# When the zeros of a score table start, and what the first gather of each beat waits for

## The chip, the cores and the metric

The kernel runs on one core of a Trainium2 chip. The metric is the device time of one execution in microseconds (us). The kernel before takes 2227.58 us, the median of three runs (2226.61 to 2228.72). Of one further execution there is a hardware profile: that execution took 2228.76 us, and 2227.0 us lie between its first and its last instruction (the span). Times within the profile count from the start of the span.

The engines are called by their short names: PE multiplies matrices (TensorE), DVE is the vector engine, ACT the scalar engine, POOL is GpSimd, and SP only starts transfers. DMAs are started from the queues of SP, ACT and POOL.

## The reference

Two layers over a graph of 625 nodes, 10000 directed edges and 1024 features. Layer 0 adds to `x` a graph attention, a linear attention and a quantised feed-forward block; layer 1 is a two-step graph aggregation, another linear attention, a softmax attention and a mixture of eight experts. The change touches only the graph attention of layer 0:

```python
loop = jnp.arange(n, dtype=edge_index.dtype)
src = jnp.concatenate([edge_index[0], loop])
dst = jnp.concatenate([edge_index[1], loop])
xl = (x @ Wl).reshape(n, H, D)          # H = 4 heads of D = 64
xr = (x @ Wr).reshape(n, H, D)
msg = xl[src] + xr[dst]
act = jnp.where(msg > 0, msg, NEG_SLOPE * msg)
e = jnp.einsum('ehd,hd->eh', act, att)
m = jax.ops.segment_max(e, dst, num_segments=n)
p = jnp.exp(e - m[dst])
denom = jax.ops.segment_sum(p, dst, num_segments=n)
alpha = p / (denom[dst] + 1e-16)
out = jax.ops.segment_sum(alpha[..., None] * xl[src], dst, num_segments=n)
out = out.reshape(n, HID)
return out @ W_up
```

Each edge needs a row of `xl` and a row of `xr` (256 numbers each), chosen by its two node numbers, and gives four scores.

## The kernel before

**The score table.** A tensor `table` in DRAM has a row of four scores for every pair of nodes. It is first filled with zeros by one DMA of 6160 KB on SP's queue (L404), out of a tile `none` that POOL has set. Each edge's four exponentiated scores are later scattered to its pair's row, and the 625 diagonal rows are written for the self loops (`self_loops`, L647, ten small DMAs on ACT's queue). When all that is done, `load_table` (L827) reads the table back in five blocks `tb`, DVE multiplies them by the edge counts `CT` (`weigh`, L841), and PE multiplies the result by the rows `xl1` (`sums`, tile `pg`).

**The projections.** For each of five blocks of 125 nodes, `left_right` (L540) multiplies the node features by `Wl` and `Wr`. ACT copies the result to `xlr` and stores its left half to `xl_d` from its own queue and its right half to `xr_d` from POOL's queue. `rows_dma` (L171) makes two DMAs of each store, for 112 and for 13 rows.

**The beats.** The edges lie in 79 columns of up to 128. Two columns make a group, so there are 40 groups, numbered 0 to 39 (the last is one column of 16 edges). `one_beat` (L684) writes out the work of one beat g:

- up to four gathers on POOL for group g: for each column j one of `xl_d` into `ga` and one of `xr_d` into `gb` (`gather`, L605). Both tiles have five buffers, so group g needs the buffers of group g-5;
- on DVE the scores of group g-4 (`score_group`, four instructions: add, L591, L592 and L594), and on ACT the exponential of group g-5;
- on POOL two scatters for group g-6 (`scatter`, L626), which stand between the gathers.

At the end, `lags[:] = 1, 1, 2` (L807) shortens these distances: from beat 36 on there are four scatters in a beat, and DVE scores up to group g-1. The scatters that are left after beat 39 follow on their own. A scatter also waits until the scatter before it has landed, since both write the table.

**The order.** PE, DVE, ACT, POOL and SP each run their instructions in the order in which the program writes them out. `work(us)` (L702) counts estimated PE time and writes out a beat whenever enough has gone by (8.6 us for a beat from beat 7 on). In between stand the two linear projections `pk`, `pv`, the count matmuls `pct`, the queries `pq` and, last, the output products `px` (`mixed`). Before the last beats DVE sums weights for the quantiser (`weight_sums`, L767), and among them it rounds the weights (`ternary`, L782 to L785).

**The pace.** `group` and the other matmul helpers note their newest matmul in `latest["pe"]` (L131). `behind` (L135) adds a semaphore wait by hand. The first gather of each beat waits with it for that matmul:

```python
                    if j == 0 and side == 0 and "pe" in latest:
                        behind(got, latest["pe"])
```

**SP's queue.** SP starts the loads of `x`, the weights `wd` and `wlr`, the biases, the two halves of `Wk`, then the zeros (L404) and the two halves of `Wv` (L121). The next transfer behind these is a bias of the second half (L237), which waits for DVE until 158 us.

Of the kernel before, what the change touches and what calls it, by code (L numbers as in the profile page):

```python
# [20 lines left out]
NT = 5  # L21
P = 125
# [20 lines left out]
def gps_kernel(tc: tile.TileContext, w: dict, out: bass.AP):  # L43

    again = attempt(tc, w, out, False)
    with tc.If(again > 0):
        attempt(tc, w, out, True)  # L50
# [3 lines left out]
def attempt(ctx: ExitStack, tc: tile.TileContext, w: dict, out: bass.AP, shifted: bool):  # L54

    nc = tc.nc
# [6 lines left out]
    def ps1(name):  # L63
        pool, n = psums[-1]
        return pool.tile([128, 512], FP, tag="ps1", name=name, bufs=n)
# [61 lines left out]
    def group(dst, pairs):  # L127

        for i, (lhsT, rhs) in enumerate(pairs):
            made = nc.tensor.matmul(dst, lhsT=lhsT, rhs=rhs, start=(i == 0), stop=(i == len(pairs) - 1))  # L130
        latest["pe"] = made.ins.name  # L131

    latest = {}

    def behind(ins, name):  # L135

        tc.add_manual_dep(ins.ins, name, mybir.DependencyInfo(mybir.DependencyClass.Sync,
                                                              mybir.DependencyReason.DATA), reason="pace")
        return ins
# [30 lines left out]

    def rows_dma(eng, dst, src):  # L171

        eng.dma_start(out=dst[0:112], in_=src[0:112])
        eng.dma_start(out=dst[112:P], in_=src[112:P])


    graph = ctx.enter_context(ExitStack())
# [41 lines left out]
    def mid(shape, name):  # L219
        return midp.tile(shape, FP, tag="mid", name=name)  # L220
# [135 lines left out]
    with ExitStack() as st0:  # L356
# [4 lines left out]
        table = dram.tile([128 * 3080, 4], FP, name="table")  # L361
# [3 lines left out]
        with ExitStack() as edges:  # L365
# [4 lines left out]

            xin = big.tile([P, NT, D], FP, tag="big", name="xin")
            rows_dma(nc.sync, xin[:, 0, :], xrows[0])

            si = pool.tile([128, EN], I32, name="si")
            di = pool.tile([128, EN], I32, name="di")
            rw = pool.tile([128, KC], FP, name="rw")
            nc.scalar.dma_start(out=rw, in_=w["rms_w"])
            rows_dma(nc.sync, xin[:, 1, :], xrows[1])
            wd = wpool.tile([128, KC, 256], FP, tag="w", name="wd")
            nc.sync.dma_start(out=wd, in_=w["W_down"].rearrange("(k p) n -> p k n", p=128))  # L380
            for t in range(2, NT):
                rows_dma(nc.sync, xin[:, t, :], xrows[t])
# [5 lines left out]
            def load_edges():  # L388
                for dst, name in ((si, "src"), (di, "dst")):
# [8 lines left out]
            none = pool.tile([128, 440], FP, name="none")  # L398
# [2 lines left out]
                                  lambda us: work(us), nc.sync)  # L401
            lin.biases(0)
            lin.wk = Half(wpool, w["L0_Wk"], 0)
            nc.sync.dma_start(out=table.rearrange("(p a b) h -> p a (b h)", p=128, a=28),  # L404
                              in_=none.unsqueeze(1).to_broadcast([128, 28, 440]))
            lin.wv = Half(wpool, w["L0_Wv"], 0)
            sf = pool.tile([128, EN], FP, name="sf")
            df = pool.tile([128, EN], FP, name="df")
            up = pool.tile([128, EN], FP, name="up")
# [88 lines left out]
            xlr = mid([P, NT, 512], "xlr")  # L498
            xl_d = dram.tile([N, 256], FP, name="xl_d")
            xr_d = dram.tile([N, 256], FP, name="xr_d")  # L500
# [39 lines left out]
            def left_right(t):  # L540
                def pe():
                    hold["pl", t] = ps1("plr")
                    xdT = hold.pop(("xdT", t))
                    group(hold["pl", t][:P], [(xdT[:, k, :], wlr[:, k, :]) for k in range(2)])

                def after():
                    nc.scalar.activation(xlr[:, t, :], hold.pop(("pl", t))[:P], AF.Identity, scale=r0[:, t:t + 1])
                    rows_dma(nc.scalar, xl_d.rearrange("(t p) e -> t p e", p=P)[t], xlr[:, t, 0:256])
                    rows_dma(nc.gpsimd, xr_d.rearrange("(t p) e -> t p e", p=P)[t], xlr[:, t, 256:512])

                do(None, pe, after)

# [52 lines left out]
            def gather(g, j, side):  # L605
                lo, n, p = groups[g]
                if j == 0 and side == 0:
                    ab[g] = [pool.tile([128, G, 256], FP, tag=k, name=k, bufs=5) for k in ("ga", "gb")]
                if j < n:
                    src, ix = ((xl_d, si), (xr_d, di))[side]  # L610
                    got = nc.gpsimd.indirect_dma_start(  # L611
                        out=ab[g][side][0:p, j, :], out_offset=None, in_=src[:, :],
                        in_offset=bass.IndirectOffsetOnAxis(ap=ix[0:p, lo + j:lo + j + 1], axis=0))
                    if j == 0 and side == 0 and "pe" in latest:
                        behind(got, latest["pe"])

            def score_group(g):
                lo, n, p = groups[g]
# [65 lines left out]
            def one_beat():  # L684
                g = beat["g"]
                beat["g"] += 1
                if 5 <= g < NT + 5:
                    self_loops(g - 5)
                if lags[1] > lags[0]:
                    raise_all(g - lags[1])  # L690
                    scores(g - lags[0])
                else:
                    scores(g - lags[0])
                    raise_all(g - lags[1])
                for j in range(G):
                    if g < len(groups):
                        gather(g, j, 0)
                        scatter(g - lags[2] - 1)
                        gather(g, j, 1)
                    scatter(g - lags[2])  # L700
# [87 lines left out]
            for m in range(KC):  # L788
# [5 lines left out]
                if m < 3:  # L794
# [3 lines left out]
                                      in_=w[("w_gate", "w_up", "w_down")[m]].rearrange("(k p) n -> p k n", p=128))  # L798
# [418 lines left out]
    for m in range(KC):  # L1217
# [8 lines left out]
        a = m % 4  # L1226
# [48 lines left out]
    for b in range(NB_MIN, NB):  # L1275
        nc.gpsimd.dma_start(out=y_d[b * 128:(b + 1) * 128, :].rearrange("p (a n) -> p a n", a=4),
                            in_=zero.unsqueeze(1).to_broadcast([128, 4, 256]))
# [694 lines left out]
```

## Time and profile before

| what | us |
|---|---|
| median of three runs | 2227.58 |
| the profiled execution | 2228.76 |
| its span | 2227.0 |
| PE busy in the span | 2112.5 (95%) |
| DVE busy | 713.3 (32%) |
| POOL busy | 341.4 (15%) |
| ACT busy | 194.1 (9%) |
| gathers into `ga`, L611, 79 of them: busy, mean of one | 79.7, 1.009 |
| gathers into `gb`, L611, 79 of them: busy, mean of one | 81.8, 1.036 |
| scatters, L631, 79 of them: busy, mean of one | 84.2, 1.066 |
| idle time of POOL just before the `ga`, the `gb` and the scatter instructions | 74.8, 25.3, 49.4 |
| mean granted clock of PE | 0.977 |

The rows on gathers and scatters count POOL's own instruction[...]; the data land later. The usual distance between two such instructions that wait for nothing is 0.30 us, so some 24 us of each 79 are such distances and not waits. PE being busy 95% of the span says that the kernel as a whole is carried by PE. It doesn't say that PE is what ends last in every stage: what an edit in one stage is worth is read from the waits of that stage.

### The profile page before, as it was taken

How to read it: one execution, taken by the hardware profiler on the slowest of the kernel's cores; microseconds unless marked ns; L12 is line 12 of the kernel's file. 1: busy time of each engine (PE TensorE's matmuls, PEld its weight loads, DVE VectorE, ACT ScalarE, POOL GpSimd, SP SyncE). 2: the span in 40 equal slices, each digit the busy share in tenths (PEclk: the TensorE clock that was granted, in tenths of full speed). 3: DMA queues.
4: the chain of work that ended last, by engine and by line, in shares of the span. 5: the costliest groups of instructions: out<-in, count | busy, mean ns of one | idle time of the engine just before them, and what ended most of it. 6: DMA issues, size and time to landing. Idle time of an engine off the chain costs nothing. (4 is left out here: it accounts for less than half of the span.)

```text
span 2227.0 us, 17363 instructions
## 1 busy us (share of the span) xinstructions
PE 2112.5 (95%) x6934; PEld 1209.9 (54%) x6934; DVE 713.3 (32%) x1214; ACT 194.1 (9%) x354; POOL 341.4 (15%) x349
## 2 busy tenths in 40 slices
PE   8899799578899999999999999999999999999998
PEld 6466375245444777754445767557744444444443
DVE  5765467557623560000113133322011111111112
ACT  2000010001211100000000111100000000000000
POOL 1666656610000020210000000110000000000011
PEclk9999899878999999999999999999999999999999
DMA  9226252071122110231213111021099987997742
GB/s 299 77 62 209 59 182 81 25 212 33 38 85 71 52 38 1 85 142 38 76 38 104 38 38 38 20 103 61 34 347 337 331 325 282 327 331 286 275 144 92
DMA packets 145848, 301.62 MB, mean 135 GB/s; under 512 B 12370, under 2 KB 22436, under 8 KB 145754
## 3 DMA queue, kind: packets, MB, share of 16 engines
q1 hardware_dynamic: 123700, 244.23, 30.7%
q0 software_dynamic: 17376, 46.42, 7.1%
q10 hardware_dynamic: 4678, 9.72, 1.4%
q8 instruction: 58, 0.95, 0.2%
q14 instruction: 36, 0.29, 0.0%
HBM read 277.49 MB, written 22.84 MB: 135 GB/s over the span
## 5 line engine op out<-in xcount | busy, mean ns | idle before, releaser
L130 PE MATMUL pu<-w,xgT 128*128 128x512 f32 x768 | 333.9, 593 | 1.9 <-DVE xgT L1266 1.9
L130 PEld LDWEIGHTS pu<-w,xgT 128*128 128x128 f32 x768 | 144.0, 190 | 174.8 <-issue 171.7
L130 PE MATMUL pyb<-w,hb 128*128 128x512 f32 x384 | 174.3, 599 | 2.5 <-ACT yb L105 2.1
L130 PE MATMUL pq<-xnT,w 128*128 128x313 f32 x512 | 139.6, 432 | 13.8 <-DVE v L286 13.0
L130 PE MATMUL pk<-w,xnT 128*125 128x512 f32 x320 | 143.2, 599 | 3.3 <-issue 2.8
L130 PE MATMUL pv<-w,xnT 128*125 128x512 f32 x320 | 142.2, 597 | 1.5 <-issue 1.1
L130 PE MATMUL p<-tT,w 128*128 128x313 f32 x512 | 136.3, 428 | 0.4 <-DVE tT L1266 0.4
L130 PEld LDWEIGHTS pq<-xnT,w 128*128 128x128 f32 x512 | 98.2, 193 | 53.5 <-DVE v L286 13.8
L130 PEld LDWEIGHTS pyb<-w,hb 128*128 128x128 f32 x384 | 69.8, 189 | 90.9 <-issue 74.8
L1806 DVE TENSOR_TENSOR su<-pu,su 128x512 f32<-128x512 f32 x24 | 16.6, 692 | 314.6 <-ACT su L1805 314.6
L130 PEld LDWEIGHTS p<-tT,w 128*128 128x128 f32 x512 | 96.8, 190 | 37.9 <-issue 1.2
L130 PEld LDWEIGHTS pk<-w,xnT 128*125 128x125 f32 x320 | 59.8, 189 | 77.0 <-issue 76.1
L130 PEld LDWEIGHTS pv<-w,xnT 128*125 128x125 f32 x320 | 59.9, 189 | 75.4 <-issue 72.6
L1789 POOL DMA_INDIRECT xg<-rows_d,slots x12 | 11.4, 946 | 524.8 <-PE pxg L1796 449.0
L631 POOL DMA_INDIRECT table<-es,at x79 | 84.2, 1066 | 49.4 <-issue 26.2
L611 POOL DMA_INDIRECT ga<-xl_d,si x79 | 79.7, 1009 | 74.8 <-issue 33.2
L611 POOL DMA_INDIRECT gb<-xr_d,di x79 | 81.8, 1036 | 25.3 <-issue 22.8
L745 PE MATMUL px<-w,oT 128*125 128x512 f32 x160 | 69.8, 594 | 2.9 <-DVE x L909 2.0
L130 PE MATMUL px<-w,hT 128*125 128x512 f32 x160 | 70.3, 592 | 0.0
L130 PE MATMUL px<-w,oT 128*125 128x512 f32 x160 | 70.3, 592 | 0.0
L130 PE MATMUL ph<-meanT,w 128*128 128x313 f32 x256 | 70.1, 426 | 0.0
L130 PE MATMUL ph<-xnT,w 128*128 128x313 f32 x256 | 70.0, 427 | 0.0
(366 smaller groups left out, 2459.9 us busy)
## 6 DMA issues: line engine op xcount, KB each, us to landing
w<-in_eW_dram SPq DMA_DIRECT2D x144, 1024.0 KB
w<-in_L_Wk_dram SPq DMA_DIRECT2D x8, 1024.0 KB
w<-in_L_Wv_dram SPq DMA_DIRECT2D x8, 1024.0 KB
w<-in_L_Wq_dram SPq DMA_DIRECT2D x8, 1024.0 KB
w<-in_L_Wo_dram SPq DMA_DIRECT2D x8, 1024.0 KB
w<-in_W_self_dram SPq DMA_DIRECT2D x8, 1024.0 KB
w<-in_W_neigh_dram SPq DMA_DIRECT2D x8, 1024.0 KB
w<-in_sW_dram SPq DMA_DIRECT2D x8, 1024.0 KB
```

The source lines that it names most:

```text
L130: made = nc.tensor.matmul(dst, lhsT=lhsT, rhs=rhs, start=(i == 0), stop=(i == len(pairs) - 1))
L611: got = nc.gpsimd.indirect_dma_start(out=ab[g][side][0:p, j, :], out_offset=None, in_=src[:, :], in_offset=bass.IndirectOffsetOnAxis(ap=ix ...
L631: nc.gpsimd.indirect_dma_start(out=table[:, :], out_offset=bass.IndirectOffsetOnAxis(ap=at[0:p, lo + j:lo + j + 1], axis=0), in_=es[0:p, l ...
L745: made = nc.tensor.matmul(hold["px", t][:P, c, :], lhsT=oT[:, k, nodes(t)], rhs=wo[c](k), start=(k == 0), stop=(k == KC - 1 and keep is no ...
L1789: nc.gpsimd.indirect_dma_start(out=xg, out_offset=None, in_=rows_d[:, :], in_offset=bass.IndirectOffsetOnAxis(ap=slots[:, b:b + 1], axis=0))
L1806: nc.vector.tensor_tensor(su, pu[:, 0, :], su, op=ALU.mult)
```

## The change

`rows_dma` returns its two DMAs. The zeros are written out behind both halves of `Wv` on SP's queue, and they wait for the four stores of the last block of nodes (two to `xl_d`, two to `xr_d`). The first gather of a beat no longer waits for the newest matmul, but for the landing of the last gather of the beat ahead; the first gather of all waits for none.

```diff
     def rows_dma(eng, dst, src):
 
-        eng.dma_start(out=dst[0:112], in_=src[0:112])
-        eng.dma_start(out=dst[112:P], in_=src[112:P])
+        return [eng.dma_start(out=dst[lo:hi], in_=src[lo:hi]) for lo, hi in ((0, 112), (112, P))]
...
             lin.wk = Half(wpool, w["L0_Wk"], 0)
-            nc.sync.dma_start(out=table.rearrange("(p a b) h -> p a (b h)", p=128, a=28),
-                              in_=none.unsqueeze(1).to_broadcast([128, 28, 440]))
             lin.wv = Half(wpool, w["L0_Wv"], 0)
+            zeros = nc.sync.dma_start(out=table.rearrange("(p a b) h -> p a (b h)", p=128, a=28),
+                                      in_=none.unsqueeze(1).to_broadcast([128, 28, 440]))
...
                     nc.scalar.activation(xlr[:, t, :], hold.pop(("pl", t))[:P], AF.Identity, scale=r0[:, t:t + 1])
-                    rows_dma(nc.scalar, xl_d.rearrange("(t p) e -> t p e", p=P)[t], xlr[:, t, 0:256])
-                    rows_dma(nc.gpsimd, xr_d.rearrange("(t p) e -> t p e", p=P)[t], xlr[:, t, 256:512])
+                    for put in (rows_dma(nc.scalar, xl_d.rearrange("(t p) e -> t p e", p=P)[t], xlr[:, t, 0:256])
+                                + rows_dma(nc.gpsimd, xr_d.rearrange("(t p) e -> t p e", p=P)[t],
+                                           xlr[:, t, 256:512])):
+                        if t == NT - 1:
+                            behind(zeros, put.ins.name)
...
                         in_offset=bass.IndirectOffsetOnAxis(ap=ix[0:p, lo + j:lo + j + 1], axis=0))
-                    if j == 0 and side == 0 and "pe" in latest:
-                        behind(got, latest["pe"])
+                    if j == 0 and side == 0 and g:
+                        behind(got, latest["gather"])
+                    latest["gather"] = got.ins.name
```

No instruction is added or taken away on any engine; the only one that changes its place is the DMA of the zeros on SP.

## The prediction

> **What bounds the kernel now.** The page's summary puts PE at 95%, and its chain of waits names only the last matmuls, so I went to PE's timeline for holes near the edited lines, then followed the largest back over DVE and POOL.
>
> PE's timeline around 400 us:
>
> ```profile
> 394.86 27.71 PE L745 MATMUL px<-w,oT 128*125 128x512 f32 x64
> 454.23 0.68 PE L130 MATMUL pg<-xl,pT 125*125 125x65 f32 x2 [31.66 <-DVE pT L841]
> ```
>
> PE ends its projections at 422.57 and stands still for 31.66 us, until DVE has weighed the first table block. DVE's timeline:
>
> ```profile
> 388.91 0.68 DVE L621 TENSOR_TENSOR ga<-ga,gb 128x512 f32<-128x512 f32 x1
> ...
> 390.35 0.69 DVE L592 TENSOR_REDUCE es<-ga 128x8 f32<-128x512 f32 x1
> ...
> 409.76 0.69 DVE L621 TENSOR_TENSOR ga<-ga,gb 128x512 f32<-128x512 f32 x1 [7.62 <-DMA gb<-xr_d,di]
> ...
> 453.14 4.84 DVE L841 TENSOR_TENSOR pT<-tb,CT 125x500 f32<-125x500 f32 x5 [16.54 <-DMA tb<-table]
> ```
>
> DVE waits for the block's landing. POOL's timeline leads back:
>
> ```profile
> 217.02 0.97 POOL L611 DMA_INDIRECT ga<-xl_d,si  x1 [0.30 <-issue]
> ...
> 384.86 0.96 POOL L611 DMA_INDIRECT ga<-xl_d,si  x1 [8.50 <-PE px L745]
> ...
> 406.84 0.97 POOL L611 DMA_INDIRECT gb<-xr_d,di  x1 [0.30 <-issue]
> ...
> 432.64 2.31 POOL L631 DMA_INDIRECT table<-es,at  x1 [1.41 <-DMA table<-es,at]
> 436.82 0.96 POOL L631 DMA_INDIRECT table<-es,at  x1 [1.88 <-issue]
> 439.18 0.96 POOL L631 DMA_INDIRECT table<-es,at  x1 [1.39 <-DMA table<-es,at]
> 442.03 0.85 POOL L631 DMA_INDIRECT table<-es,at  x1 [1.90 <-issue]
> 444.54 0.90 POOL L173 DMA_DIRECT2D tb<-table  x1 [1.66 <-issue]
> ```
>
> So from 384.86 (the first gather of beat 36) to 444.54 POOL is the bound, and behind that hole everything follows the table: a microsecond on POOL's last scatter is one on the whole. Before 422 it is the other way round: PE has some 30 us to spare against POOL.
>
> **What the Trainium skill says.** "DMA: Bandwidth & Descriptors", section "Anatomy of one DMA", prices a DMA from POOL at about 2.0 us fixed plus its bytes, most of it the wait for the last write's receipt, and says that waits happen on the issuing sequencer. The trace agrees: the gather at 406.84 ends at 407.81, and DVE starts on it 1.95 us later. "SWDGE vs HWDGE vs iDMA" says that one DMA engine takes turns between queues, and that POOL's descriptors suffer from DVE's two-port modes; POOL's instructions of 1.5 to 2.3 us lie where DVE rounds weights (423 to 436). "TensorE: Matmul & The Clock Gate", Part 1, says that an idle PE drops to half rate; the windows show clock 0.56 at 422 to 454 and 0.50 at 454 to 470, so this rides on the hole and moves with it.
>
> **The change part by part.**
>
> *Zeros.* SP's and ACT's timelines before:
>
> ```profile
> 20.84 0.62 SPq L404 DMA_DIRECT2D table<-none  x1
> 39.30 5.45 SPq L121 DMA_DIRECT2D w<-in_L_Wv_dram  x2
> 52.19 0.31 ACTq L174 DMA_DIRECT2D xl_d<-xlr  x1
> 71.52 0.31 ACTq L173 DMA_DIRECT2D table<-own  x1
> ```
>
> The last store to `xl_d` shared a semaphore with the zeros and sat from about 46.3 until 52.19; it landed at 55.97 by the packet records, and POOL's first gather came at 57.64. Now the store takes a semaphore behind `Wv`, issues at 46.3, lands near 50, and the first gather comes at about 51.5: 6 us earlier. PE's `pv` at 55.88 waited for no load, so the earlier `Wv` gives nothing. The zeros issue near 51.5, take about 22 us (6.3 MB; 23.4 us before, from first to last packet, at 379 GB/s in all), and land at about 76. Behind them on SP stands a bias due at 158: free. ACT's diagonal store at 71.52 waits for them, some 5 us; ACT's next due work is at 81.40, so it is free, and POOL's first scatter isn't due until about 100. Bounds: nothing, up to a few us on PE if the zeros last past 81, which the later hole swallows. While they run, gathers land later: 2.7 us after POOL's end (bounds 1.5 and 4.5, what stores lagged under load), against 1.46 in quiet (packet records).
>
> *The PE wait removed.* 13 first gathers waited more than 0.34 us, summing to 45.0 us (8.50 the largest, 5.43 at 295.72); less 0.30 each, 41 us. That is what POOL gets back up to beat 36.
>
> *The landing wait added.* POOL's reaction is priced by its scatters: packets land 0.76 us after a scatter's end, the next starts 1.41 after that end when it is the only wait, and 1.88 to 1.92 when another wait is listed behind it. So POOL wakes 0.65 or 1.15 after landing. From beat 6 on, the program as built lists the landing first and DVE's buffer wait behind it: 1.46 + 1.15 = 2.61 us from the last gather's end to the next beat. A scatter stood there already: 0.30 + 0.99 + 0.30 = 1.59. Net +1.02 a beat. Unpaced beats ran 7.96 to 8.29 us (from 209.00 to 217.02: 8.02), so now 9.08.
>
> *The sum to beat 36.* Beats 0 to 2 under the zeros: four gathers, 5.0, plus 2.7 + 0.65 = 8.3 each; beats 3 to 5 about 7.1. Beat 6 starts at 51.5 + 25 + 21.5 = 98 (91.63 before). Thirty beats of 9.08 are 272. At 166 to 196, 287 to 303, near 317 and 360 weight loads fill the DMA engines (0.99 and 0.93 in the windows) and landings take 3.5 to 5 us (packet records): about four beats pay 3.3 more, 13. Beat 36 at 383, between 377 and 388, against 384.86: a gain of 2. The 41 us are nearly all given back.
>
> *The tail.* Beat 37 needs the buffers of group 32, free at 391.04, so it can't start before 391.3 (396.72 before): no gain over 5.4. From beat 36 at 383 it comes at 383 + 11.86 + 1.0 = 395.9. Beats 38 and 39 pay 1.0 each, of which the scatter chain's own 0.65 us wait behind them absorbs part: +0.8 together. The block load now lists more waits behind its scatter: +0.6 (0 to 1.2). End of table: -2 + 1 + 0.8 + 0.6 = +0.4, that is nothing. DVE scores a group four beats after its gathers, some 35 us, so it isn't held up before the tail.
>
> **The rivals.**
>
> *Unchanged (likeliest).* The PE pace goes and the landing wait takes its place at the same size: 2228.76 + 0.4, about 2229 in the profile's terms, which stands 1.2 above the median; 2227.9 beside the runs. Own range 2223 to 2232.
>
> *Faster.* POOL wakes in 0.65 rather than 1.15, or its instructions suffer less from DVE: beat 36 at about 368, and the tail stands on group 32's buffer at 391.3. Gain 5.4, less 0.2 to 1.4 for the tail; or 1.5 more, if the 1.51 us stall at 401.36 that the trace doesn't explain is gone. 2221 to 2223. For it: the wait price comes from scatters. Against: it repeats in eight scatters.
>
> *Slower.* POOL becomes landing-bound throughout: each 0.1 us more in a beat is 3 us at the end, undamped. Beyond 9.25 us a beat the end is later by over 4.5. A second wait priced behind the landing (+0.5 a beat, 15 us, less the 2 in hand), or more beats ending under weight loads at 3.3 each, give 2232 to 2242; centre 2237. For it: no slack is left once the beat takes 9.1 and the mean pace of PE was (384.86 - 91.63)/30 = 9.77.
>
> That the change doesn't do what it says would be a landing long over when POOL arrives; 2.61 against 1.59 excludes it.
>
> **How the numbers follow.** Unchanged 0.44, faster 0.26, slower 0.30. What this kernel's measurement can tell from no change is about 0.2%, 4.5 us. The unchanged case reaches over its own border a little on both sides, which these chances contain. The range goes from 2221.5, near the floor that group 32 sets, to 2238, leaving out the worst third of the slower case.
>
> **What would show it.** First gather near 51.5; first scatter of beat 6 near 100; beats of about 9.1 us with "DMA gb" in place of "PE" before first gathers; beat 36 between 377 and 388; PE's hole ending within 4 us of 454. A hole ending at 448 to 450 with beat 37 at 391 is the faster case; beat 36 past 390 is the slower. A PE or ACT wait for the zeros that is still felt after 100 would make the reasoning wrong.

## The result, and the profile after

| | before | after |
|---|---|---|
| median of 20 runs, us | 2226.66 (2223.11 to 2232.17) | 2231.60 (2227.45 to 2235.50) |
| the profiled execution, its span | 2228.76, 2227.0 | 2234.13, 2232.4 |
| first gather of beat 0 | 57.64 | 49.67 |
| first gather of beat 6 | 91.63 | 100.07 |
| first gather of beat 36 | 384.86 | 386.15 |
| load of the first table block, `tb` | 444.54 | 446.50 |
| end of PE's hole | 454.23 | 456.11 |

The ratio of the medians is 1.0021, 95% interval 1.0013 to 1.0028: 4.9 us slower, at the border of what this kernel's measurement tells from no change. Line numbers of the kernel after are 2 (gathers) or 3 higher than before from the beats on.

POOL's timeline after (start, duration, engine, line, instruction; in brackets the idle time before it and what ended it):

```profile
49.67 1.02 POOL L613 DMA_INDIRECT ga<-xl_d,si  x1 [1.79 <-DMA xr_d<-xlr]
...
61.34 0.95 POOL L613 DMA_INDIRECT ga<-xl_d,si  x1 [6.79 <-DMA gb<-xr_d,di]
...
70.85 0.94 POOL L613 DMA_INDIRECT ga<-xl_d,si  x1 [4.81 <-DMA gb<-xr_d,di]
...
377.62 0.96 POOL L613 DMA_INDIRECT ga<-xl_d,si  x1 [1.22 <-DMA gb<-xr_d,di]
...
386.15 0.96 POOL L613 DMA_INDIRECT ga<-xl_d,si  x1 [1.22 <-DMA table<-es,at]
...
446.50 1.55 POOL L173 DMA_DIRECT2D tb<-table  x2 [1.75 <-DMA table<-es,at]
```

The first gather comes 8 us earlier. Then beats 1 and 2 stand 6.79 and 4.81 us for landings, because the zeros now run under them; later the wait is about 1.2 us a beat. From beat 6 to beat 36 a beat takes (386.15 - 100.07)/30 = 9.54 us.

PE's timeline after:

```profile
401.05 15.89 PE L748 MATMUL px<-w,oT 128*125 128x512 f32 x32 [7.69 <-DVE kept L755]
456.11 0.68 PE L130 MATMUL pg<-xl,pT 125*125 125x65 f32 x2 [39.18 <-DVE pT L844]
```

PE ends its projections at 416.94, 5.6 us earlier than before, although it stood 7.69 us for DVE just ahead; the hole ends 1.9 us later. The spans differ by 5.4 us, so 3.5 us more arise behind the table. They are found by lining up PE's matmuls by number. Some 0.6 us come at 521. The other 3.0 us come at one place, shown here in PE's timeline before and then after:

```profile
618.19 1.08 PE L130 MATMUL pdn<-dn,room 128*125 128x512 bf16 x4 [2.95 <-DVE room L993]
619.11 7.03 PE L130 MATMUL pv<-w,xnT 128*125 128x512 f32 x16
```

```profile
620.70 1.97 PE L130 MATMUL pdn<-dn,room 128*125 128x512 bf16 x4 [2.95 <-DVE room L996]
622.46 9.17 PE L130 MATMUL pv<-w,xnT 128*125 128x512 f32 x16
```

The wait ahead is the same 2.95 us, but the same matmuls took 0.89 and 2.14 us longer: PE's granted clock (the share of its full rate) in the windows from 600 to 640 is 0.96 before and 0.87 after. The Trainium skill, "TensorE: Matmul & The Clock Gate", Part 1, says that the activity window behind the clock runs freely, so that the number of slow matmuls varies from run to run; the trace agrees in so far as the same wait cost nothing in one execution and 3.0 us in the other. From the end of the hole to the end of the span the fourteen profiles of this study take 1772.7 to 1776.3 us; the profile before is near the bottom (1772.8) and the one after at the top, so the 3.5 us are most likely chance of the execution and not the change.

### The profile page after: what moved, and what is told of

Read it like the earlier page. It is cut to its first block, busy times and chain, and to the rows that moved or that the text cites. A ratio compares the mean times of both kernels' runs of the same rounds, so it can differ in the third digit from the quotient of the medians.

```text
span 2232.4 us, 17367 instructions
## 1 busy us (share of the span) xinstructions
PE 2114.9 (95%) x6934; PEld 1212.6 (54%) x6934; DVE 712.2 (32%) x1214; ACT 193.9 (9%) x354; POOL 338.0 (15%) x349
## 5 line engine op out<-in xcount | busy, mean ns | idle before, releaser
L130 PE MATMUL pg<-xl,pT 125*125 125x65 f32 x200 | 32.0, 332 | 41.5 <-DVE pT L844 40.2
```

## The experiments

**Four kernels that take the change apart.** They ran on a chip on which the kernel before took 2227.59 us (16 runs).

Early zeros, PE's pace kept (against the changed kernel):

```diff
-                    if j == 0 and side == 0 and g:
-                        behind(got, latest["gather"])
-                    latest["gather"] = got.ins.name
+                    if j == 0 and side == 0 and "pe" in latest:
+                        behind(got, latest["pe"])
```

> The zeros behind Wv and behind the projections' stores, as in the changed kernel, but the first gathers wait for PE's work as they did before. Theory A (the landing wait alone decides, 0.93 us a beat, and the zeros are free): the early start is eaten by PE's pace long before beat 36, so beat 36 starts within 1.5 us of 384.9, PE's hole ends within 1.5 us of 454.2 and the time is that of before within 2 us. Theory B (the zeros, now running under the first gathers, whose landings took 4 to 6 us there, cost the 4.9 us): slower than before by 3 to 5 us, beat 36 at 387 or later.

Measured: 2221.47 us, ratio to before 0.9972 (0.9962 to 0.9981), 6 us faster. Beat 36 starts at 375.34, the hole ends at 444.46. Both theories fall: the earlier start isn't eaten by PE's pace, for PE itself ends its projections 9.5 us earlier in the profiled execution, which was the fastest of the ten.

The landing wait, zeros in their old place (against the kernel before):

```diff
-                    if j == 0 and side == 0 and "pe" in latest:
-                        behind(got, latest["pe"])
+                    if j == 0 and side == 0 and g:
+                        behind(got, latest["gather"])
+                    latest["gather"] = got.ins.name
```

> The zeros where they were, the landing wait in place of PE's. Theory A: without zeros under them, beats 0 to 5 take 7.1 us each from 57.6, so beat 6 starts at 57.6 + 42.7 = 100.3, the same as the 100.1 of the changed kernel, and the rest is the same: time equal to the changed kernel within 2 us (about 5 above before), PE's hole ends at 456 within 1.5 us. Theory B (zeros cost): the time falls back to that of before, within 2 us. Theory C (the early zeros are worth their 6 to 8 us of earlier start and are what nearly pays for the landing wait): 6 us or more above the changed kernel, beat 6 at 106 or later.

Measured: 2235.31 us, 1.0032 (1.0021 to 1.0044). Beat 6 starts at 98.15, not 100.3, because the first gather, free of PE's pace, came at 55.31. B and C fall, and A misses too: it allowed 2 us beside the changed kernel, and the time is 3.7 above it. The landing wait is what costs: 7.7 us here.

No wait made by hand (against the changed kernel):

```diff
-                    if j == 0 and side == 0 and g:
-                        behind(got, latest["gather"])
-                    latest["gather"] = got.ins.name
```

> The changed kernel without any wait made by hand on the first gathers: what is left are the five buffers. Theory A (POOL's chain bounds the table from the start, and each beat pays 0.93 us to the landing): 36 beats give up to 33 us at beat 36, cut by what DVE holds in buffers; beat 36 between 355 and 375, PE's hole ends between 430 and 446, time 2207 to 2222. Rival (gathers of two beats in flight slow each other, or another wait takes the same place): beat 36 at 384 or later, time within 3 us of the changed kernel or above it.

Measured: 2258.88 us, 1.0142 (1.0121 to 1.0162). Theory A is wrong by some 40 us. POOL's timeline of this kernel:

```profile
329.07 0.96 POOL L613 DMA_INDIRECT ga<-xl_d,si  x1 [11.34 <-DVE es L596]
...
384.27 0.96 POOL L613 DMA_INDIRECT ga<-xl_d,si  x1 [13.86 <-DVE es L596]
```

POOL runs ahead and then stands for buffers that DVE hasn't freed, since DVE is late. PE's own waits, all between 56 and 450 (sum, count, longest):

```profile
PE pct L466 <- issue: 13.8, 17, 1.7
PE pkv L130 <- issue: 12.6, 9, 2.4
PE pq L130 <- ACT qf L331: 12.5, 1, 12.5
```

"issue" means that PE waited for nothing that the profile shows. PE, which carries the whole kernel, loses 35 us in such pauses (all its "issue" rows together), and 16.3 more standing for ACT. This turned the study: are there such pauses before, too?

Two beats ahead (against the changed kernel):

```diff
-                    if j == 0 and side == 0 and g:
-                        behind(got, latest["gather"])
-                    latest["gather"] = got.ins.name
+                    if j == 0 and side == 0 and g >= 2:
+                        behind(got, latest["gather", g - 2])
+                    latest["gather", g] = got.ins.name
```

> The changed kernel with each beat's first gather behind the landing of the last gather two beats ahead, which in quiet landed 7 us before. Theory A (the cost is the time from POOL's end to the landing plus the waking): it is gone, and the time is that of the kernel without waits, within 2 us. Rival (what costs is one more wait listed on the instruction, whether it is over or not, about 0.5 us): half of the 0.93 us a beat stays, 15 us above the kernel without waits at beat 36.

Measured: 2247.21 us, 1.0093 (1.0077 to 1.0109), with PE pauses of 23.5 us. Neither theory spoke of what decided it.

**The pauses.** PE's timeline of the kernel before shows them, between 77 and 104 us:

```profile
77.06 0.29 PE L467 MATMUL pct<-ring 128*125 128x313 bf16 x1 [0.89 <-issue]
77.79 0.29 PE L467 MATMUL pct<-ring 128*125 128x313 bf16 x1 [0.43 <-issue]
...
101.03 0.59 PE L130 MATMUL pk<-w,xnT 128*125 128x512 f32 x1 [0.81 <-issue]
102.44 0.59 PE L130 MATMUL pk<-w,xnT 128*125 128x512 f32 x1 [0.82 <-issue]
```

One matmul every 0.70 or 1.40 us, where 16 such `pk` matmuls otherwise take 7.03. The "issue" rows of PE's waits sum to 13.5 us here; the same view of the changed kernel has none. They aren't the whole loss. Behind them comes one long wait, shown here in PE's and DVE's timelines:

```profile
252.29 7.03 PE L130 MATMUL pv<-w,xnT 128*125 128x512 f32 x16
272.33 10.21 PE L130 MATMUL pq<-xnT,w 128*128 128x313 f32 x32 [13.01 <-DVE v L286]
```

```profile
271.59 0.69 DVE L286 TENSOR_TENSOR v<-pv,bv_t 125x512 f32<-125x512 f32 x1 [12.73 <-remote]
```

PE stands for DVE's `v`, but `v` reads `pv`, which PE ended at 259.32 by the record. DVE stood idle and began 12.3 us after that ("remote" means that the profile names no releaser). So not only PE is late: DVE is late behind a result that PE's record shows as done.

So four more kernels were run; their chip turned out to be another one, on which the kernel before took 2197.88 us (17 runs).

The kernel before once more, with no edit:

> The kernel before once more, unchanged, for a second profile. PE lost 4.6 us at 77 to 83 and 8.5 us at 100 to 110 to pauses in which it waited for nothing that the profile shows, while the changed kernel lost nothing there. Theory S (these pauses belong to a POOL that issues gathers without a break, and come with it each time): pauses of 5 us or more in sum between 60 and 240 again, though not at the same places. Rival (chance of one execution): under 2 us.

Measured: 2200.71 us in its one execution. The rival's number came, no pause at all, but it doesn't show chance, for the chip was another. With the pauses 28 us are gone, and so is the long wait: DVE starts `v` 0.04 us behind the end of that `pv`, and PE stands 0.78 us for it. The same stretch of PE's timeline:

```profile
77.74 7.03 PE L130 MATMUL pv<-w,xnT 128*125 128x512 f32 x16
84.60 4.16 PE L467 MATMUL pct<-ring 128*125 128x313 bf16 x30
88.60 7.03 PE L130 MATMUL pk<-w,xnT 128*125 128x512 f32 x16
```

Between 76 and 110 PE gains 13.5 us on the first profile, matmul by matmul. POOL's waits for PE, in its waits between 50 and 400, first in the first profile:

```profile
POOL ga L611 <- PE pq L130: 12.2, 4, 5.4
...
POOL ga L611 <- PE px L745: 8.5, 1, 8.5
...
POOL ga L611 <- PE pv L130: 3.7, 2, 3.4
POOL ga L611 <- PE pk L130: 2.7, 1, 2.7
POOL ga L611 <- PE pct L467: 2.6, 1, 2.6
```

and in the second:

```profile
POOL ga L611 <- PE px L745: 2.5, 1, 2.5
...
POOL ga L611 <- PE pct L467: 0.9, 3, 0.3
...
POOL ga L611 <- PE pq L130: 0.6, 2, 0.3
```

A PE that isn't late hardly holds POOL at all. Beat 36 starts at 355.53 instead of 384.86.

The landing wait in beats 7 to 19 only (against the changed kernel):

```diff
-                    if j == 0 and side == 0 and g:
+                    if j == 0 and side == 0 and 7 <= g < 20:
                         behind(got, latest["gather"])
+                    elif j == 0 and side == 0 and "pe" in latest:
+                        behind(got, latest["pe"])
                     latest["gather"] = got.ins.name
```

> The early zeros, the landing wait for beats 7 to 19 only, and PE's pace for the beats before and behind them. Theory S (POOL's unbroken stream makes PE pause, PE's pace hands the loss on to POOL, and the landing wait breaks the stream): the landing wait costs nothing in beats 7 to 19, which PE's pace held to 219.9 for beat 20 anyway; PE's pauses there, 6 us in the kernel with early zeros alone, are gone, so that behind 220 it runs 5 us or more ahead of that kernel; beat 36 at 367 to 371, time 2213 to 2218. Rival (the pauses have nothing to do with POOL's stream): pauses as before, time 2221 within 2 us. Rival (a landing wait costs 0.93 us a beat wherever it stands): 13 beats, 12 us, 2230 or more.

Measured on this chip: 2200.20 us, 1.0012 (1.0003 to 1.0021). Its question couldn't be answered where nothing pauses. But it prices the landing wait in thirteen beats: beat 36 starts at 354.02, against 348.86 with early zeros and PE's pace alone (the run further down).

The landing wait twice in a beat (against the changed kernel):

```diff
-                    if j == 0 and side == 0 and g:
+                    if side == 0 and (g or j):
```

> The changed kernel with the second column's first gather behind the landing of the gather ahead of it too: a second landing wait of about 1.0 us in each beat. Theory A (POOL's chain sets the table from beat 6 on, nothing gives the waits back): 30 beats by 1.0 us, beat 36 at 415 to 420, PE's hole ends at 486 to 494, time 2260 to 2270. Rival (the landing wait also frees something that pays for it, so that a second one pays too): less than 15 us above the changed kernel. PE's pauses without a visible wait stay under 2 us in both.

Measured: 2261.87 us (1.0288, 1.0271 to 1.0304); beat 36 at 416.13, the hole ends at 485.17. Theory A's numbers came, and the part that holds is that with a landing wait POOL's chain sets the end. Its sum, thirty beats by 1.0 us, is luck: beat 6 is already 13.7 us later than in the changed kernel (113.78), because the second wait too stands under the zeros, and the thirty beats behind give 0.54 each (10.08 against 9.54 us).

No landing wait in beats 36 to 39 (against the changed kernel):

```diff
-                    if j == 0 and side == 0 and g:
+                    if j == 0 and side == 0 and 0 < g < 36:
```

> The changed kernel without the landing wait for beats 36 to 39, where POOL alone is the bound. Theory A (a landing wait is 0.93 us on POOL's chain): beat 36 at 386 less 0.9, hole ends 2.5 to 3.7 us earlier, at 452.4 to 453.6, time 2228 to 2229. Rival (each scatter of the tail waits for the landing of the one before it anyway and takes up what is gained): the hole ends within 1 us of 456.1.

Measured: 2230.78 us (1.0140, 1.0123 to 1.0156), the hole ends at 453.30. That is the number of theory A, but not for its reason: against the changed kernel's profile from a chip without pauses (next runs) the way from beat 36 to the block load shrinks only from 60.45 to 59.15 us. Four waits that are 0.93 us longer cost 1.3; the scatters' own waits take up the rest, as the rival says.

**The same kernels without pauses.** On a third chip, kernel before 2198.79 us (42 runs); no new edits.

> The changed kernel once more, because the kernel before has two times: 2227 on one chip, where PE pauses while POOL gathers without a break, and 2198 on a second, where it doesn't. Theory S (the landing wait keeps POOL's chain, which no PE pause reaches, so its time is the same on both chips, while the kernel before loses 29 us to the pauses on one of them): 2230 to 2236 on any chip; so beside a kernel before of 2198 the change costs 32 to 37 us, 1.5%, and beside one of 2227 it costs 5. Rival (the second chip is faster for all kernels): 2198 plus 5, 2203.

> The changed kernel without waits made by hand on the first gathers, once more. Theory S (its 2259 came from PE's pauses, which it provokes most): on a chip where the kernel before takes 2198 there are no pauses, POOL runs beats of 8.0 to 8.5 us from 49 on, beat 36 at 335 to 355, time 2180 to 2198; on one where it takes 2227, 2250 to 2265 again. Rival (the buffers, or gathers that crowd each other, make it slow): above 2240 on any chip.

> Early zeros with PE's pace, once more. On a chip where the kernel before takes 2227: 6 us under it, as the first time. Where it takes 2198: theory S says that there PE's pace binds POOL hardly at all (one wait of 2.5 us ahead of beat 36), so that the 5 us of earlier start last to the end: 3 to 6 us under it, 2192 to 2195. Rival (the gain of 6 us was fewer pauses of PE, not the earlier start): within 2 us of it.

| | where before took 2227 | where before took 2199 | ratio there |
|---|---|---|---|
| changed kernel | 2231.60 | 2231.27 | 1.0150 (1.0133 to 1.0167) |
| no wait by hand | 2258.88 | 2190.90 | 0.9967 (0.9959 to 0.9975) |
| early zeros, PE's pace | 2221.47 | 2193.30 | 0.9978 (0.9971 to 0.9984) |

All three came out where theory S put them. The changed kernel has one time on both kinds of chip; the others gain 28 to 68 us where PE doesn't pause. The pauses alone don't make up that gain: the "issue" rows of these two kernels were 6.1 and 35.3 us. The rest fits late starts like that of `v`, which reach 10.2 and 19.5 us in their first profiles. The kernel without waits, POOL's timeline there:

```profile
80.85 1.19 POOL L613 DMA_INDIRECT ga<-xl_d,si  x1 [0.30 <-DVE gs L651]
...
405.99 1.55 POOL L173 DMA_DIRECT2D tb<-table  x2 [1.76 <-DMA table<-es,at]
```

and that of the changed kernel on the same chip:

```profile
60.65 0.94 POOL L613 DMA_INDIRECT ga<-xl_d,si  x1 [6.66 <-DMA gb<-xr_d,di]
...
99.90 0.95 POOL L613 DMA_INDIRECT ga<-xl_d,si  x1 [2.56 <-issue]
...
384.64 0.96 POOL L613 DMA_INDIRECT ga<-xl_d,si  x1 [1.23 <-DMA table<-es,at]
...
445.09 1.55 POOL L173 DMA_DIRECT2D tb<-table  x2 [1.76 <-DMA table<-es,at]
```

This pair prices the landing wait with nothing else in the way. At beat 6 it has cost 19.1 us (99.90 against 80.85), at beat 36, which starts at 346.4 without it, 38.3, and at the block load 39.1. Half of it arises in beats 0 to 5, while the zeros run, and 0.64 us a beat in the thirty beats behind; the time differs by 40.4.

The middle landing wait was tried once more on a fourth chip, in the hope of one that pauses:

> Early zeros, the landing wait for beats 7 to 19, PE's pace elsewhere, once more, to find a chip on which PE pauses. If the kernel before takes 2227 here: theory S says that a POOL stream broken once a beat leaves PE unpaused in those beats, so beat 36 comes before 371 and the time is 2200 to 2216; the rival (what stops the pauses isn't the break) says 2219 to 2223, the time with early zeros alone. If it takes 2198 here, it tells only how well 2200 repeats: 2198 to 2202, because the first time the 13 landing waits put beat 36 at 354.0 where early zeros alone had 348.9.

Measured: 2199.96 us beside 2196.63 (19 runs), 1.0011 (1.0001 to 1.0020). Beat 36 starts at 355.94. It repeats, and tells no more: whether breaking POOL's stream for some beats stops the pauses stays open.

## Why the prediction was right, and where it wasn't

- **The total.** Forecast 2227.9 (unchanged), measured 2231.6, in the forecast's own range but over its middle by 3.7. In the profiled executions 1.9 us of the difference stand at the end of the hole and 3.5 behind it, most likely chance of the execution; how the medians divide isn't shown. The claim that the half clock "rides on the hole and moves with it" left out that PE's clock can differ elsewhere.
- **The landing chain.** Forecast for beat 6: 98, measured 100.07. For thirty beats: 272 + 13 = 285, measured 286.1. Beat 36: 383, measured 386.15. The first term was short by 4 us (beats 0 to 5 took 50.4 instead of 46.5): landings under the zeros were taken at 2.7 us behind POOL's end, with bounds of 1.5 and 4.5. By the packet records the seven gathers under the zeros took 4.1 to 6.1 (median of all from 50 to 75 us: 4.8). The earlier first gather, 49.67 instead of 51.5, gave 1.8 back.
- **The thirty beats.** The sum for these was right to 1 us, but by luck, for two errors cancelled. The 24 beats without a long landing took 8.83 us in the mean, not 9.08, which takes off 6.0: beats without a wait for PE go down to 7.64 in the profile before, not 7.96. Six beats, not four, took over 11 us, 19.7 over 9.08 instead of 13. And the wait, priced at 1.02 a beat, costs 0.64 in the pair on the third chip.
- **"The zeros: free".** Right in that no wait of PE or ACT for them was felt. But with the landing wait they aren't free: they are most of the 19 us lost by beat 6. With PE's pace they are a gain of 5 to 6 us, on both kinds of chip.
- **"PE has some 30 us to spare before 422".** This step failed. The same text had beat 36 waiting 8.50 us for PE, so PE's lateness went straight into POOL's chain and the table. The runs show it twice: with early zeros PE released beat 36 9.5 us earlier and the hole ended 9.8 us earlier; without pauses the hole ended 29.4 us earlier.
- **"41 us of PE waits is what POOL gets back".** As a sum over this profile it was right. But the waits were PE's lateness on this chip, from its pauses and from DVE's and ACT's late starts, handed on to POOL, and not a pace that was set too slow: without them three rows with 4.0 us are left. There the change gives nothing back, and costs 32.5 us.
- **The tail.** Forecast +2.4 from beat 36 to the block load, measured 60.35 against 59.68, +0.7. The floor at 391.3, where beat 37 would wait for group 32's buffer, isn't fixed: it hangs on DVE, and DVE moves with PE. With early zeros and PE's pace beat 37 started at 387.20 on the pausing chip, and without any wait at 358.3 on the third. So the faster case was cut off at a false limit. The mechanism itself is real: without waits POOL did stand for DVE's buffers on the pausing chip.
- **The slower case** named the right mechanism, a POOL bound by landings throughout. It came about; in the comparison the PE waits that fell away paid for most of it.

## What to carry to other kernels

Before a wait by hand is priced as a cost, ask why the engine it waits for is late: a short "issue" gap between single matmuls, repeated over 10 us, is lost time of the bottleneck, even if each gap is below 1 us. Compare, too, when a result is done by the record with when its reader starts. A wait for a landing in a loop of DMAs costs in every pass (0.64 us a beat here), and more while a large transfer runs (19.1 us in the first six beats). And if a kernel's time hangs on such gaps, compare on more than one chip: of the four kernels timed on both kinds the one without waits went from last place to first.

The version with early zeros and PE's pace beats both kernels on both kinds of chip, by 0.28% and 0.22% against the one before. Without any wait by hand it is 2.4 us faster still where PE doesn't pause, and 37 us slower where it does.

## What the runs showed of the hardware

- PE can pause without any visible cause: one matmul every 0.70 or 1.40 us. On the chip of the first four experiments it did so in all three of their kernels without a landing wait one beat back, for 6.1, 35.3 and 23.5 us by the "issue" rows of PE's waits between 56 and 450, and 13.5 us in the first profile of before. The kernels with that wait in every beat have no such row on any chip, and on the three other chips no kernel has one. That the wait's gap in POOL's stream is what prevents the pauses is a likely reading, but the cause isn't shown. It isn't slower DMAs: by the packet records the gathers landed 1.47 us behind POOL's end in the first profile of before and 1.45 in the second (medians from 75 to 110 us). Nor was it told apart whether the chip itself or the place of the program in its memory makes the difference.
- In the same four profiles DVE or ACT start late behind a result that PE's record shows as done: at most by 12.3 us in the first profile of before, and by 10.2, 19.5 and 23.9 with early zeros, without a wait and two beats ahead. With the landing wait in every beat the most is 2.2 us (changed kernel) and 1.9 (zeros in their old place); on the other chips the same starts come some 0.04 us behind.
- Those six profiles, the two with the landing wait among them, also lack records of the semaphore signals by which the engines wait for each other: 950 to 1005 for DVE, where all eight of the other chips have 1048. So something differs in that setting for every kernel. Whether signals are held up, PE itself stands, or the recording plays a part wasn't tested; a wait whose signal has no record is also one that "issue" or "remote" would be written beside.
- Without pauses the kernel before is 1.3 to 1.4% faster on three chips (2196.63 to 2198.79) than on the one of the experiments (2227.59).
- While 6.3 MB of zeros are written, a gather's data land 4.1 to 6.1 us behind POOL's end (the seven that the changed kernel made between 50 and 67 us), against 1.46 in quiet.
